# Moving first-layer statistics from VectorE to ScalarE and GpSimd, and a recurrence's cell update to ScalarE

## The chip, the cores and the metric

The kernel runs on one core of one Trainium2 chip. The metric is the time of one execution on the device, in microseconds (us). Five engines of the core work side by side, each through its own instructions in order: TensorE (PE in the profile, its weight loads PEld), VectorE (DVE), ScalarE (ACT), GpSimd (POOL), and SyncE (SP), which here only issues transfers (DMA). An engine that has to wait for another holds up everything queued behind the waiting instruction.

## The reference

The input `x` has 16 images of 128 channels and 64 x 64 points. Two layers are added to it, each after a group normalisation: a diagonal LSTM (a recurrence along the anti-diagonals of the image), and a small simulated quantum circuit on each point. Only the beginning of the first layer matters here.

```python
def _gn(v, G=32, eps=1e-5):
    B_, C_, H_, W_ = v.shape
    g = v.reshape(B_, G, C_ // G, H_, W_)
    m = jnp.mean(g, axis=(2, 3, 4), keepdims=True)
    s = jnp.var(g, axis=(2, 3, 4), keepdims=True)
    return ((g - m) / jnp.sqrt(s + eps)).reshape(v.shape)
...
def step(carry, ist):
    h, c = carry
    h_shift = jnp.pad(h, ((0, 0), (0, 0), (1, 0)))[:, :, :-1]
    s_s = (jnp.einsum('oi,bih->boh', w_ss[:, :, 0], h_shift)
           + jnp.einsum('oi,bih->boh', w_ss[:, :, 1], h) + b_ss[None, :, None])
    gates = ist + s_s
    ofi = jax.nn.sigmoid(gates[:, :3 * C])
    o, f, ig = (ofi[:, :C], ofi[:, C:2 * C], ofi[:, 2 * C:])
    g = jnp.tanh(gates[:, 3 * C:])
    c_new = f * c + ig * g
    h_new = o * jnp.tanh(c_new)
    return ((h_new, c_new), h_new)
...
x = x + _L0_conv_ref(_gn(x), L0_conv_w_is, L0_conv_b_is, L0_conv_w_ss, L0_conv_b_ss)
x = x + _L1_conv_ref(_gn(x), L1_conv_pre_w, L1_conv_pre_b, L1_conv_q_weights, L1_conv_post_w, L1_conv_post_b)
```

So two things must be there before the recurrence can use the images: the mean and variance of every image and group of four channels, and the state of the rows that are not reached yet. A row of the skewed image that waits for its first point sees zeros as input, and its state is the same for every image; it depends only on the weights and on the number of steps.

## The kernel before

The kernel has a preparation, a scan over the diagonals (the LSTM), and a last stage (the circuit and the output). The scan and the last stage are not touched by the change. The preparation loads the 16 images one after another. Of each image, the first 40 rows go to the resident `ring` and the other 24 to seven small buffers (`rest`, three, and four of the `spare` tiles), in pieces of 512 elements per channel (`CHUNK`): eight pieces an image, numbered k = 0 to 7, where k = 0 to 4 lie in the ring.

The order of the work on every engine is the order of the program, since the preparation runs under a hand-written schedule (`manual_schedule`). The parts are these:

- **Statistics** (`statistics`, L285 to L287): one VectorE instruction per piece writes six numbers per channel into `stats` (two halves with count, mean and sum of squared deviations). `aggregated` (L289) makes a mean and a variance per channel of the eight pieces, once per image, into `mv1`.
- **Rounds of the waiting rows** (`inv_step`, L191 to L212): 33 rounds (`EARLY`), each dependent on the one before. TensorE multiplies the state with the summed weights, one product per gate (L199); ScalarE activates the four gates in the order forget, input, candidate, output (L202); GpSimd makes the new cell in three instructions (forget gate times cell L205, input gate times candidate L206, sum L207); ScalarE takes its tanh (L209) and multiplies it with the output gate (L210), which gives the next state `hinv`. Behind each round TensorE has two products whose result nobody reads (`keep`, L182): they only keep it busy, the first of them reads a piece of image b.
- **The loop over images** (L375 to L396) runs two or three rounds per image, then issues the transfers of image b + 2, the statistics of image b + 1 (ring) and of image b (rest), and the aggregation of image b.
- **The seam to the scan** (L400 to L430): GpSimd copies the waiting rows' state into the scan's first state (L402, L403). TensorE then runs, in order, the first gate products of the scan (L408, eight of them in the trace), three products that keep it busy (L416), the mean over each group (L147, from `mv1`), another such product, and the mean of the variances (L426). VectorE and ScalarE form the reciprocal root (L154 to L158), GpSimd normalises the first diagonals (L576 to L588), and the scan starts.

Preparing the circuit's coefficients (`coefficients`, L312 to L319, seven GpSimd instructions) stands ahead of five memsets of the state tiles and one of `w_image` in GpSimd's order. The tile `w_amp` is filled with the circuit's amplitudes later, during the scan, and is not used before.

Of the kernel before, what the change touches and what calls it, by code (L numbers as in the profile page):

```python
# [11 lines left out]
F32 = mybir.dt.float32  # L12
AF = mybir.ActivationFunctionType
# [3 lines left out]
P = 128  # L17
NB = 16
NH = 64
NW = 64  # L20
SLOTS = 32
# [4 lines left out]
BLOCK = ROWS * NW  # L26
CHUNK = 2 * BLOCK
EARLY = 33
FIRST = 8
STRIP = 4  # L30
FEW = 96
# [10 lines left out]
GO, GF, GI, GG = 0, 1, 2, 3  # L42
FUNC = {GO: AF.Sigmoid, GF: AF.Sigmoid, GI: AF.Sigmoid, GG: AF.Tanh}
# [38 lines left out]
def kernel(  # L82
# [16 lines left out]
    nc = tc.nc  # L99
# [36 lines left out]
    def place(r):  # L136

        return (r + AHEAD if r < SLOTS else r - SLOTS) * NW
# [22 lines left out]
    with ExitStack() as scan:  # L161
# [17 lines left out]
        def keep(pool, tag, v):  # L179

            ps = pool.tile([P, v.shape[-1]], F32, name=nc.get_next_instruction_name(), tag=tag)
            nc.tensor.matmul(ps, lhsT=wsT[:, 0:P], rhs=v, start=True, stop=True)  # L182
# [8 lines left out]
        def inv_step(j, pool):  # L191


            ps = {}
            rhs = hinv[:, j : j + 1].to_broadcast([P, P])
            for g in ORDER:
                ps[g] = pool.tile([P, P], F32, name=f"inv_ps{j}_{g}", tag=f"inv{g}")
                w = wsT[:, g * 128 : (g + 1) * 128]
                nc.tensor.matmul(ps[g], lhsT=w, rhs=rhs, start=True, stop=True)  # L199
            ac = small.tile([P, 4], F32, name=f"inv_a{j}", tag="inv_a")  # L200
            for g in ORDER:
                nc.scalar.activation(ac[:, g : g + 1], ps[g][:, 0:1], FUNC[g], bias=bias[:, g : g + 1])  # L202
            ig = small.tile([P, 2], F32, name=f"inv_i{j}", tag="inv_i")
            c = cinv[:, j + 1 : j + 2]
            nc.gpsimd.tensor_mul(ig[:, 0:1], ac[:, GF : GF + 1], cinv[:, j : j + 1])  # L205
            nc.gpsimd.tensor_mul(ig[:, 1:2], ac[:, GI : GI + 1], ac[:, GG : GG + 1])  # L206
            nc.gpsimd.tensor_add(c, ig[:, 0:1], ig[:, 1:2])  # L207
            th = small.tile([P, 1], F32, name=f"inv_t{j}", tag="inv_t")
            nc.scalar.activation(th, c, AF.Tanh)  # L209
            nc.scalar.activation(  # L210
                hinv[:, j + 1 : j + 2], th, AF.Identity, scale=ac[:, GO : GO + 1]
            )  # L212

        def above(v, a, b):

# [4 lines left out]
        with ExitStack() as prep:  # L220
# [64 lines left out]
            def statistics(b, k):  # L285
                v = ring[:, b, k * CHUNK : (k + 1) * CHUNK] if k < 5 else rests[b][k - 5]
                nc.vector.bn_stats(stats[:, b, k, :], v)  # L287

            def aggregated(b):  # L289
                nc.vector.bn_aggr(  # L290
                    mv1[:, b, :], stats[:, b, 0:8].rearrange("p g s -> p (g s)")
                )


            q3 = qw.rearrange("p (n a) -> p a n", a=3)
            ang = pp.tile([P, 2, 3, 8], F32, name="ang")
            rnd = pp.tile([P, 2, 3, 8], F32, name="rnd")
# [14 lines left out]
            def coefficients():  # L312
                nc.gpsimd.tensor_mul(co[:, 0], trig[:, 0, 0, :], trig[:, 0, 2, :])
                nc.gpsimd.tensor_mul(co[:, 1], trig[:, 1, 0, :], trig[:, 0, 2, :])
                nc.gpsimd.tensor_mul(co[:, 2], trig[:, 0, 1, :], trig[:, 1, 2, :])
                nc.gpsimd.tensor_mul(co[:, 3], trig[:, 1, 1, :], trig[:, 1, 2, :])
                nc.gpsimd.tensor_scalar_mul(co[:, 4:8], co[:, 0:4], -1.0)
                nc.gpsimd.tensor_copy(cur[:, 0], expand)
                nc.gpsimd.memset(cur[:, 1], 0.0)  # L319
# [41 lines left out]
                nc.vector.tensor_add(sum_n[:, 2 * i : 2 * i + 2], v[:, :, 0::2], v[:, :, 1::2])  # L361
            transposed("wsT", wsT, lambda g: sum_n[:, g, :])
            biases()
            coefficients()
            for v in (*hst, *xns, none):
                nc.gpsimd.memset(v, 0.0)
            nc.gpsimd.memset(w_image, 0.0)

            for k in (3, 4, 0):
                statistics(0, k)  # L370


            between = [angle_weights, output_weights]
            done = 0
            for b in range(NB):  # L375
                while b < NB - 1 and done * (NB - 1) < EARLY * (b + 1):
                    inv_step(done, ps_inv)
                    keep(ps_keep, "keep", ring[:, b, CHUNK : CHUNK + P])
                    keep(ps_keep, "keep", wsT[:, 0:P])
                    if done == 0:  # L380

                        transposed("wxT", wxT, lambda g: wx_n[:, g, :])
                        transposed("w0T", w0T, lambda g: ws_n[g // 2][:, g % 2, 0::2])
                        transposed("w1T", w1T, lambda g: ws_n[g // 2][:, g % 2, 1::2])
                    elif done > 4 and between:
                        between.pop(0)()
                    done += 1
                if b + 2 < NB:
                    rows(b + 2)
                if b + 1 < NB:  # L390
                    behind(b + 1)
                    for k in ORDERED:
                        statistics(b + 1, k)
                for k in (5, 6, 7):
                    statistics(b, k)
                aggregated(b)  # L396
            prep_ps.close()


# [499 lines left out]
        with tc.manual_schedule():  # L899
# [42 lines left out]

            nc.scalar.activation(warm, shift, AF.Sin)


            def image_weights(i0, i1):
                nc.vector.tensor_mul(
                    w_image[:, i0:i1, 16:32],
# [231 lines left out]
```

## Time and profile before

Three runs took 1410.7, 1411.99 and 1412.01 us, median 1411.99. The profiled execution took 1411.93 us, of which the profile's span is 1409.8 us.

| | busy us | share of the span |
|---|---|---|
| TensorE | 1355.0 | 96% |
| VectorE | 975.5 | 69% |
| GpSimd | 887.6 | 63% |
| ScalarE | 776.0 | 55% |

The page divides the span into 40 slices of about 35 us; a digit is a busy share in tenths. The first three slices are the preparation: transfers at nine tenths in the first two and GB/s of 339, 407 and 234, then almost none until the middle of the scan. A share of busy time over the whole span says nothing about the preparation, whose limits are its own, so it is read in shorter stretches. Among the groups of instructions in the first 125 us, the rounds show as 132 gate activations (mean 262 ns), 33 tanh (203 ns), 33 products with the output gate (294 ns) on ScalarE, and 99 GpSimd instructions of 189 to 193 ns; the statistics as 128 VectorE instructions of 674 to 681 ns and 16 aggregations of 372 ns.

When reading such lines: the time in a line is from the start of its first instruction to the end of its last; the bracket gives the idle time of that engine just before and the instruction that ended it. Neighbouring instructions on ScalarE and GpSimd overlap in the records a little.

### The profile page before, as it was taken

How to read it: one execution, taken by the hardware profiler on the slowest of the kernel's cores; microseconds unless marked ns; L12 is line 12 of the kernel's file. 1: busy time of each engine (PE TensorE's matmuls, PEld its weight loads, DVE VectorE, ACT ScalarE, POOL GpSimd, SP SyncE). 2: the span in 40 equal slices, each digit the busy share in tenths (PEclk: the TensorE clock that was granted, in tenths of full speed). 3: DMA queues.
4: the chain of work that ended last, by engine and by line, in shares of the span. 5: the costliest groups of instructions: out<-in, count | busy, mean ns of one | idle time of the engine just before them, and what ended most of it. 6: DMA issues, size and time to landing. Idle time of an engine off the chain costs nothing.

```text
span 1409.8 us, 20064 instructions
## 1 busy us (share of the span) xinstructions
PE 1355.0 (96%) x6046; PEld 967.6 (69%) x6046; DVE 975.5 (69%) x2541; ACT 776.0 (55%) x1852; POOL 887.6 (63%) x1599
## 2 busy tenths in 40 slices
PE   6778999999999999999999999999999999999995
PEld 5658977777777766666677767777776787886332
DVE  7973565566665666887777776666665567876996
ACT  4655666555555555555555555555555566654331
POOL 4225777777777766777777776777777677763300
PEclk9999999999999999999999999999999999999998
DMA  9960000000000000133333100000000000014999
GB/s 339 407 234 2 1 1 1 1 0 1 0 1 1 1 1 1 60 120 120 120 120 120 60 1 1 1 1 0 1 1 0 1 0 1 1 31 143 383 400 358
DMA packets 64075, 107.04 MB, mean 76 GB/s; under 512 B 5040, under 2 KB 32720, under 8 KB 63968
## 3 DMA queue, kind: packets, MB, share of 16 engines
q1 hardware_dynamic: 59328, 94.39, 18.5%
q0 software_dynamic: 3408, 10.58, 2.0%
q8 instruction: 48, 0.79, 0.2%
q10 hardware_dynamic: 1232, 0.80, 0.2%
q14 instruction: 59, 0.48, 0.1%
HBM read 59.61 MB, written 46.14 MB: 75 GB/s over the span
## 4 chain that ended last, share of the span: by engine, by line
PE 82%; DVE 4%; ACT 1%; issue 1%; POOL 1%; DVEq 0%; ACTq 0%; POOLq 0%
PE ps L783 46%; PE ps L597 28%; PE po_None L1062 3%; PE theta_None L1011 2%; PE am_None L1040 1%; DVE spare L868 1%; DVE ps L858 1%; DVE ps L798 0%; DVE cst L861 0%; DVE stats L732 0%; ACT g L862 0%; ACT g L802 0%; PE po L1062 0%; DVE cst L850 0%; DVE ring L1080 0%
## 5 line engine op out<-in xcount | busy, mean ns | idle before, releaser
L597 PE MATMUL ps<-spare,wxT 128*128 128x512 f32 (+18 forms) x1280 | 479.7, 518 | 0.6 <-POOL spare L588 0.6
L798 DVE TENSOR_TENSOR ps<-ps,both 128x256 f32<-128x256 f32 (+9 forms) x536 | 219.1, 410 | 301.1 <-PE ps L783 299.5
L802 ACT ACTIVATE ps<-ps,bias 128x512 f32<-128x512 f32 (+23 forms) x480 | 279.1, 583 | 221.1 <-DVE ps L798 184.8
L783 PE MATMUL ps<-spare,w1T 128*128 128x256 f32 (+16 forms) x1272 | 346.8, 354 | 9.6 <-DVE spare L759 5.0
L597 PEld LDWEIGHTS ps<-spare,wxT 128*128 128x128 f32 x1280 | 231.1, 190 | 173.0 <-issue 155.4
L783 PE MATMUL ps<-spare,w0T 128*128 128x256 f32 (+16 forms) x1272 | 344.0, 352 | 0.0
L833 ACT COPY both<-ps 128x256 f32<-128x256 f32 (+9 forms) x536 | 189.6, 356 | 181.3 <-PE ps L783 161.7
L783 PEld LDWEIGHTS ps<-spare,w1T 128*128 128x128 f32 x1272 | 230.6, 190 | 36.5 <-DVE spare L868 7.2
L783 PEld LDWEIGHTS ps<-spare,wsT 128*128 128x128 f32 x1088 | 196.1, 190 | 80.4 <-DVE spare L868 30.1
L783 PE MATMUL ps<-spare,wsT 128*128 128x256 f32 (+14 forms) x1088 | 243.9, 366 | 2.6 <-DVE spare L868 1.2
L783 PEld LDWEIGHTS ps<-spare,w0T 128*128 128x128 f32 x1272 | 230.5, 190 | 21.0
L641 POOL TENSOR_TENSOR ring<-ring,spare 128x256 f32<-128x256 f32 (+15 forms) x375 | 231.5, 644 | 17.9 <-DVE spare L868 17.9
L588 POOL TENSOR_TENSOR spare<-spare,rstd 128x512 f32<-128x512 f32 (+10 forms) x160 | 170.9, 1068 | 14.8 <-DVE rstd L158 2.3
L582 POOL TENSOR_TENSOR spare<-ring 128x256 f32<-128x256 f32 (+13 forms) x165 | 139.8, 847 | 0.0
L862 ACT ACTIVATE g<-cst 128x256 f32<-128x256 f32 (+20 forms) x320 | 102.9, 368 | 65.5 <-DVE cst L861 65.1
L868 DVE TENSOR_TENSOR spare<-g,ps 128x256 f32<-128x256 f32 (+17 forms) x319 | 105.3, 368 | 44.8 <-ACT g L862 40.2
L576 POOL TENSOR_TENSOR spare<-ring,mean 128x256 f32<-128x256 f32 (+15 forms) x191 | 122.9, 644 | 5.6 <-DVE mean L148 5.4
L631 POOL TENSOR_TENSOR spare<-spare 128x240 f32<-128x240 f32 (+9 forms) x136 | 102.7, 755 | 36.4 <-DVE spare L868 32.8
L888 POOL COPY spare<-spare 128x16 f32<-128x16 f32 x64 | 21.0, 329 | 150.9 <-DVE spare L868 150.9
L802 ACT ACTIVATE g<-ps,bias 128x512 f32<-128x512 f32 (+20 forms) x160 | 97.3, 608 | 26.6 <-DVE ps L798 20.5
L861 DVE TENSOR_TENSOR cst<-cst,ps 128x256 f32<-128x256 f32 (+20 forms) x320 | 104.6, 368 | 5.5
L858 DVE TENSOR_TENSOR ps<-ps,g 128x512 f32<-128x512 f32 (+20 forms) x160 | 95.0, 594 | 18.8 <-ACT g L802 18.2
(370 smaller groups left out, 1096.4 us busy)
## 6 DMA issues: line engine op xcount, KB each, us to landing
out_dram<-ring SPq DMA_DIRECT2D x93, 256.0 KB, 4.8
ring<-in_x_dram SPq DMA_DIRECT2D x32, 512.0 KB, 7.6
low<-ring SPq DMA_DIRECT2D x6, 2048.0 KB, 7.5
ring<-in_x_dram SPq DMA_DIRECT2D x6, 2048.0 KB, 8.1
spare<-in_x_dram SPq DMA_DIRECT2D x27, 256.0 KB, 6.3
rest<-in_x_dram SPq DMA_DIRECT2D x21, 256.0 KB, 6.4
ring<-low POOLq DMA_DIRECT2D x18, 256.0 KB, 6.7
ring<-in_x_dram SPq DMA_DIRECT2D x16, 256.0 KB, 7.1
```

The lines of the kernel that those rows point to most:

```text
L576: op = nc.gpsimd.tensor_sub(by_pairs(xn, 0, j0, j1), x0, over(mean1, j1 - j0))
L582: op = nc.gpsimd.tensor_sub(by_pairs(xn, 1, j0, j1), lower, of)
L588: nc.gpsimd.tensor_mul(v, v, r)
L597: nc.tensor.matmul(ps[g][:, :, a:b], lhsT=wxT[:, g * 128 : (g + 1) * 128], rhs=xns[t % 2][:, :, a:b], start=t > 0, stop=True, skip_group_c ...
L641: op = engine.tensor_add(x1, x1, by_pairs(new, q, j0, j1))
L783: nc.tensor.matmul(out, lhsT=w[:, g * 128 : (g + 1) * 128], rhs=rhs, start=False, stop=True, skip_group_check=True,)
L798: nc.vector.tensor_add(v, v, both[g][:, a:b])
L802: nc.scalar.activation(to[:, :, a:w], ps[g][:, :, a:w], FUNC[g], bias=bias[:, g : g + 1])
L833: nc.scalar.copy(both[g][:, a:b], ps[g][:, 0, a:b])
L858: nc.vector.tensor_mul(ig, ig, act[GG][:, :, a:w])
L861: nc.vector.tensor_add(c[:, q], c[:, q], ig[:, q])
L868: nc.vector.tensor_mul(new[:, q, a:v], th[:, q, a:v], act[GO][:, q, a:v])
```

## The change

1. In a round, GpSimd keeps one instruction, forget gate times old cell (`kept`), issued right after the forget gate. The new cell is one ScalarE activation: candidate, scaled by the input gate, plus `kept` as bias.
2. The first product that keeps TensorE busy behind a round reads the weights in place of the image.
3. Of images 1 to 4 (`aside`), the statistics of piece k = 0 (rows 32 to 39) are made by ScalarE (`moments_of`): two activations with a running sum (x0 - x and its square, x0 being the first element; their result goes to a PSUM tile that nobody reads), and one that writes the mean into `stats`. GpSimd makes the sum of squared deviations of it.
4. Images 1 to 12 are aggregated by GpSimd, four at a time (`gathering`), in a generator: one piece of one or two instructions after each round (`some`), and whatever is left after the loop. VectorE aggregates images 0, 13, 14 and 15. The scratch space is `w_amp`.
5. `coefficients()` is called behind the memsets and the first statistics.

```diff
@@ inv_step
             ac = small.tile([P, 4], F32, name=f"inv_a{j}", tag="inv_a")
+            kept = small.tile([P, 1], F32, name=f"inv_k{j}", tag="inv_k")
+            c = cinv[:, j + 1 : j + 2]
+            th = small.tile([P, 1], F32, name=f"inv_t{j}", tag="inv_t")
+
+            def activate(to, v, func, **of):
+                nc.scalar.activation(to, v, func, **of)
+
             for g in ORDER:
-                nc.scalar.activation(ac[:, g : g + 1], ps[g][:, 0:1], FUNC[g], bias=bias[:, g : g + 1])
-            ig = small.tile([P, 2], F32, name=f"inv_i{j}", tag="inv_i")
-            c = cinv[:, j + 1 : j + 2]
-            nc.gpsimd.tensor_mul(ig[:, 0:1], ac[:, GF : GF + 1], cinv[:, j : j + 1])
-            nc.gpsimd.tensor_mul(ig[:, 1:2], ac[:, GI : GI + 1], ac[:, GG : GG + 1])
-            nc.gpsimd.tensor_add(c, ig[:, 0:1], ig[:, 1:2])
-            th = small.tile([P, 1], F32, name=f"inv_t{j}", tag="inv_t")
-            nc.scalar.activation(th, c, AF.Tanh)
-            nc.scalar.activation(
-                hinv[:, j + 1 : j + 2], th, AF.Identity, scale=ac[:, GO : GO + 1]
-            )
+                activate(ac[:, g : g + 1], ps[g][:, 0:1], FUNC[g], bias=bias[:, g : g + 1])
+                if g == GF:
+                    nc.gpsimd.tensor_mul(kept, ac[:, GF : GF + 1], cinv[:, j : j + 1])
+            activate(c, ac[:, GG : GG + 1], AF.Identity, scale=ac[:, GI : GI + 1], bias=kept)
+            activate(th, c, AF.Tanh)
+            activate(hinv[:, j + 1 : j + 2], th, AF.Identity, scale=ac[:, GO : GO + 1])
@@ behind aggregated
+            entries = stats[:, :, 0:8].rearrange("p b g (h s) -> p b (g h) s", s=3)
+            aside = range(1, 1 + GATHER)
+            sums1 = w_amp[:, 1, 0 : 2 * NB].rearrange("p (k i) -> p k i", i=NB)
+            gathered, within = (
+                w_amp[:, 0, k * P // 2 : (k + 1) * P // 2].rearrange("p (i e) -> p i e", i=GATHER)
+                for k in range(2)
+            )
+
+            def moments_of(b):
+                at = place(SLOTS)
+                v, x0 = ring[:, b, at : at + CHUNK], ring[:, b, at : at + 1]
+                junk = ps_small.tile([P, CHUNK], F32, name=f"junk{b}", tag="small")
+                for k, func in enumerate((AF.Identity, AF.Square)):
+                    nc.scalar.activation(
+                        junk, v, func, bias=x0, scale=-1.0, accum_out=sums1[:, k, b : b + 1]
+                    )
+                nc.scalar.activation(
+                    entries[:, b, 0:2, 1],
+                    sums1[:, 0, b : b + 1].to_broadcast([P, 2]),
+                    AF.Identity,
+                    bias=x0,
+                    scale=-1.0 / CHUNK,
+                )
+
+            def gathering(b0):
+                b1 = b0 + GATHER
+                pair = [P, GATHER, 2]
+                means, inners = entries[:, b0:b1, :, 1], entries[:, b0:b1, :, 2]
+                s1, s2 = (sums1[:, k, b0:b1] for k in range(2))
+                if b0 in aside:
+                    nc.gpsimd.tensor_mul(s1, s1, s1)
+                    nc.gpsimd.tensor_scalar_mul(s1, s1, -0.5 / CHUNK)
+                    yield
+                    nc.gpsimd.tensor_scalar_mul(s2, s2, 0.5)
+                    nc.gpsimd.tensor_add(
+                        inners[:, :, 0:2], *(v.unsqueeze(2).to_broadcast(pair) for v in (s1, s2))
+                    )
+                    yield
+                m, var = (mv1[:, b0:b1, k] for k in range(2))
+
+                def total(to, v):
+                    n = 8
+                    while n > 1:
+                        nc.gpsimd.tensor_add(gathered[:, :, 0:n], v[:, :, 0:n], v[:, :, n : 2 * n])
+                        v, n = gathered, n // 2
+                        yield
+                    nc.gpsimd.tensor_add(to.unsqueeze(2), v[:, :, 0:1], v[:, :, 1:2])
+                    nc.gpsimd.tensor_scalar_mul(to, to, 1.0 / 16)
+                    yield
+
+                yield from total(m, means)
+                nc.gpsimd.tensor_sub(gathered, means, m.unsqueeze(2).to_broadcast([P, GATHER, 16]))
+                nc.gpsimd.tensor_mul(gathered, gathered, gathered)
+                yield
+                nc.gpsimd.tensor_scalar_mul(within, inners, 1.0 / BLOCK)
+                nc.gpsimd.tensor_add(gathered, gathered, within)
+                yield
+                yield from total(var, gathered)
@@ the preparation
             biases()
-            coefficients()
             for v in (*hst, *xns, none):
                 nc.gpsimd.memset(v, 0.0)
             nc.gpsimd.memset(w_image, 0.0)
             for k in (3, 4, 0):
                 statistics(0, k)
+            coefficients()
             between = [angle_weights, output_weights]
             done = 0
+            behind_pool = []
+
+            def some():
+                for later in behind_pool[:1]:
+                    if next(later, True) is not None:
+                        behind_pool.pop(0)
+
             for b in range(NB):
                 while b < NB - 1 and done * (NB - 1) < EARLY * (b + 1):
                     inv_step(done, ps_inv)
-                    keep(ps_keep, "keep", ring[:, b, CHUNK : CHUNK + P])
+                    some()
+                    keep(ps_keep, "keep", wsT[:, 0:P])
                     keep(ps_keep, "keep", wsT[:, 0:P])
...
+                if b in aside:
+                    moments_of(b)
                 if b + 2 < NB:
                     rows(b + 2)
                 if b + 1 < NB:
                     behind(b + 1)
                     for k in ORDERED:
-                        statistics(b + 1, k)
+                        if k or b + 1 not in aside:
+                            statistics(b + 1, k)
                 for k in (5, 6, 7):
                     statistics(b, k)
-                aggregated(b)
+                if b in (0, *range(13, NB)):
+                    aggregated(b)
+                if b in (5, 9, 13):
+                    behind_pool.append(gathering(b - GATHER))
+            for later in behind_pool:
+                for _ in later:
+                    pass
             prep_ps.close()
```

More of the change, by code (lines that the diff above doesn't have):

```diff
@@ L28 @@
 EARLY = 33
+GATHER = 4
 FIRST = 8
```

## The prediction

> **What bounds the kernel now.** The page first: TensorE is busy 96% of the span and the chain that ended last is 82% TensorE, nearly all of it the scan (L783, L597). The change touches only the preparation before the scan, so I cut the first 150 us into stretches of 10 us. Columns: stretch, its length, then busy us (and instructions) of PE, PEld, DVE, ACT and POOL, granted clock, DMA share, GB/s.
>
> ```profile
> 80.00:90.00 10.00, 7.86 (x51) 6.25 (x50) 9.93 (x19) 5.86 (x25) 2.66 (x14) 1.00 1.04 402
> 90.00:100.00 10.00, 8.02 (x48) 5.66 (x46) 4.48 (x9) 4.64 (x15) 1.60 (x10) 1.00 0.10 37
> ```
>
> Up to 90 us the transfers (1.04) and VectorE (9.93 of 10) both look full. Which of them does the scan wait for? The timeline of each engine at the seam answers (start us, us, engine, line, operation, then idle before it and who ended that):
>
> ```profile
> 94.17 0.37 DVE L290 BATCH_NORM_AGGREGATE mv<-stats 128x2 f32<-128x48 f32 x1
> 100.91 0.17 DVE L148 TENSOR_SCALAR mean<-gm 128x16 f32<-128x16 f32 x1 [6.36 <-PE gm L147]
> ...
> 93.55 0.93 ACT L202 ACTIVATE inv_a<-inv_ps,bias 128x1 f32<-128x1 f32 x4 [0.58 <-PE inv_ps L199]
> 94.83 0.20 ACT L209 ACTIVATE inv_t<-cinv 128x1 f32<-128x1 f32 x1 [0.35 <-POOL cinv L207]
> 95.07 0.29 ACT L210 ACTIVATE hinv<-inv_t,inv_a 128x1 f32<-128x1 f32 x1
> ...
> 93.95 0.19 POOL L205 TENSOR_TENSOR inv_i<-inv_a,cinv 128x1 f32<-128x1 f32 x1 [1.54 <-ACT inv_a L202]
> 94.33 0.19 POOL L206 TENSOR_TENSOR inv_i<-inv_a 128x1 f32<-128x1 f32 x1 [0.19 <-ACT inv_a L202]
> 94.61 0.19 POOL L207 TENSOR_TENSOR cinv<-inv_i 128x1 f32<-128x1 f32 x1
> 94.73 0.20 POOL L402 COPY spare<-hinv 128x16 f32<-128x16 f32 x1
> 95.42 0.19 POOL L402 COPY spare<-hinv 128x1 f32<-128x1 f32 x1 [0.49 <-ACT hinv L210]
> 95.54 0.18 POOL L403 COPY spare<-hinv 128x1 f32<-128x1 f32 x1
> ...
> 94.46 0.49 PE L182 MATMUL I-1329_1330<-wsT 128*128 128x128 f32 x2
> 95.78 0.49 PE L408 MATMUL ps<-spare,w1T 128*128 128x128 f32 x2 [0.83 <-POOL spare L403]
> 97.67 0.81 PE L182 MATMUL I-1369_1370<-rest,wsT 128*128 128x384 f32 x2
> 100.48 0.40 PE L147 MATMUL gm<-mv,wide_sb 128*128 128x16 f32 x2
> ```
>
> VectorE ends at 94.54 and then stands idle 6.36 us: its results enter at the group mean (L147), which TensorE reaches only after the first gate products (L408) and three keep-warm products. That row of TensorE is released by POOL's copies (L403), these by the last round of the waiting rows (L210, ended 95.36). So neither VectorE nor the transfers set the seam; the 33 rounds do. From 21 us on they run with a period of 2.39 us (93.55 against 91.16), one engine after another, and the copies behind them are the gate to the scan. VectorE has about 6 us of slack.
>
> **What the skill says.** The Trainium skill, "ScalarE: Activation LUTs", section "What ACT_TABLE_LOAD costs": 186 ns for an ACTIVATE with immediates, 93 ns more for each pointer operand, 0.833 ns an element, neighbours overlapping by 93 ns. The trace agrees: L209 203 ns, L210 with a pointer scale 294 ns. "TensorE: Matmul & The Clock Gate", Part 1: after a whole idle window of about 3.4 us the array runs at half rate until it has been busy for such a window. Here the eight products of the first round took 2.05 us and those of later rounds 1.16, which fits; no gap later in the run shows a falling back, and the clock column reads 1.00 throughout. "GPSIMD Engine Reference", section 7: reads with a stride over 8 bytes cost about half more per element; at 32 elements the strided L711 (258 ns) against L712 (238) shows it to be small.
>
> **The change, part by part.**
>
> VectorE loses 12 of 16 aggregations (372 ns each, 4.5 us) and 4 of 128 statistics (0.67, 2.7 us): 7.2 us, all in slack. Worth 0. If the rounds were not there it would be worth at most the 3 us or so by which VectorE trails the last transfer.
>
> The round. Before, counted from the start of the forget gate's activation: gates at 0, 0.22, 0.45, 0.67, the last ending at 0.93; POOL's L206 at 0.78, L207 at 1.06, tanh at 1.28. After, the cell is a ScalarE activation behind the fourth gate. In order, it starts about 0.09 before that ends, at 0.84 (the third gate's result is there at 0.71, POOL's one product at 0.60). With scale and bias both pointers it takes 203 + 2 x 91 = 385 ns, an estimate from L209 and L210; end 1.22, tanh at 1.26. Gain 0.02 a round; if the second pointer is free 0.12; if the wait reaches to the fourth gate's end it is 0.10 lost. I take 0.03: 32 rounds, 1 us (bounds: 4 gained, 3 lost). Round 0 gains nothing, since POOL's memsets hold it to 15.2 us; the coefficients move behind these memsets, but their seven instructions stay ahead of round 0 in POOL's queue, so the sum is the same. The first keep-warm product now reads the weights in place of the image: same shape, its wait for a transfer shows no idle time before, 0.
>
> The piece of four images on ScalarE. Each adds two 128x512 activations with sums and a 128x2 one, queued between a round's hinv and the next round's gates, which everything waits for. The nearest row, L1031 (SBUF, 128x512), is 630 ns; with the pointer bias about 0.72. First from 0.20 after hinv's start to 0.92, second (it waits for the first) 0.96 to 1.68, third to 1.88; the next gates start at 1.77 in place of 0.87. TensorE is then ahead, gates follow at 0.15 (as in round 0: four in 0.72) and 0.2 comes back: 0.7 net. Three times 0.7, and 1.1 for the image behind the w_out copy, where there is no idle time to use: 3.2 us. Reading out a sum is not in this trace: between 0 and 0.2 us each; eight of them, I take 0.2 in all. 3.4 us (bounds 2 and 5). The images landed long before, so no wait on transfers.
>
> POOL's aggregation. The generators give out one piece a round, and POOL is idle 1.5 us in each, so during the rounds it is hidden: two instructions (0.75 us) end before the next product is due. But there are three generators of 12, 10 and 10 pieces and, from round 15 on, 18 rounds. The rest is emptied after the loop: in POOL's order 21 instructions stand behind the last round's product and ahead of the copies L402 and L403 (L482, L483 after). Their times from the rows L711 to L715 and the small ones: two scalings of 64 at 0.368, four of 64 at 0.318, three of 32 at 0.245, three of 16 at 0.225, three of 8 at 0.20, six of 4 at 0.19: 5.2 us. 18 wait for the one before, with the 0.085 seen between L206 and L207: 1.5; three overlap by 0.05. Together 6.5 us. The last product ends at 93.55 + 0.59 = 94.14, so POOL is free at 100.7 and the copies end at 101.1, not 95.72: 5.4 us later (bounds 4.5 and 6.5). Queued behind them is L408, and behind that the whole seam on TensorE, in order. What was cheap on VectorE lies bare on POOL.
>
> TensorE idles meanwhile: from 94.95 to 101.1, 6.2 us in place of 0.83. By the skill's window a gap over 3.4 us can drop the rate by half; a free-running window fits whole in 6.2 us with a chance of about 0.8. The seam after it is dense TensorE work, so 3.4 to 6.8 us at half rate lose half of that, 1.7 to 3.4. I take 2.2; bounds 0 and 3.4.
>
> **Sum.** -1 + 3.4 + 5.4 + 2.2 = +10.0 us, all before the scan. On the profiled execution (1411.93 us, span 1409.8 and 2.1 around it) that is 1421.9; the median of the three runs is 1411.99, the same for this purpose, so 1422.
>
> **Rivals.** (a) Tail bare, rest mild: rounds gain their full 4 us, the sums cost 2.5, no half rate: -4 + 2.5 + 5.4 = +4, 1416. For it: no trace here shows the array slowing after a gap. Against: two pointers have their price. (b) Nothing in sum: rounds at 2.2 us (-6) pay for the sums and a tail of 4: about 1412. The in-order start behind the fourth gate speaks against it. (c) The other side: VectorE, full for 55 us, is the true bound, the last statistics let the seam begin, and the tail is hidden behind it. Then 7.2 us less VectorE work, limited by the last transfers (0.10 of the stretch from 90 us, so about 91), brings 2 to 4 us: 1409. The price is VectorE's 0.37 per aggregation, and it decides once VectorE's end lies later than TensorE's arrival at L147. The 9.93 of 10 speaks for it, the 6.36 us of idle time ahead of L148 against. That the work isn't moved at all is excluded by the order of instructions: 4 aggregations remain on VectorE.
>
> **Chances.** Forecast 0.62 (1417 to 1427), (a) 0.17 (1414 to 1417), (b) 0.11, (c) 0.10. A measurement of this kernel tells about 0.2% (2.8 us) from no change: slower 0.77 (the forecast and most of (a)), same 0.13, faster 0.10. The range for 8 in 10 is 1413.5 to 1427.
>
> **What would show it.** Right: POOL works 6 to 7 us after its last product of the rounds; TensorE's first gate products follow the copies after a gap near 6 us, and their eight take over 2.5 us in place of 1.9; four gaps of 1.5 us or more between rounds on ScalarE; VectorE's wait at the group mean grows from 6.4 to over 14 us. Wrong: a round well under 2.3 us, or copies that end within 2 us of the last hinv; then the time is 1412 or less.

## The result, and the profile after

The kernel with the change took 1421.88 us in the median of six runs (1420.85 to 1423.0), the kernel before 1411.38 us beside it. The ratio is 1.0075, with a 95% interval of 1.0062 to 1.0088: 10.5 us slower, as forecast (1422). The profiled execution took 1421.59 us, its span 1419.8 us, against 1411.93 and 1409.8 before.

The stretch of 10 us at the seam, of the kernel after (columns as in the prediction: busy us and instructions of PE, PEld, DVE, ACT, POOL, then granted clock, DMA share, GB/s):

```profile
100.00:110.00 10.00, 5.59 (x20) 4.21 (x20) 0.00 (x0) 0.00 (x0) 3.43 (x15) 0.66 0.00 0
```

Between 100 and 110 us VectorE and ScalarE do nothing at all, GpSimd works a third of the time, and TensorE runs for part of it at a granted clock of 0.66. The timeline of the kernel after, by engine, says why (start us, us, engine, line, operation; in brackets the idle time before and who ended it):

```profile
94.23 0.37 DVE L293 BATCH_NORM_AGGREGATE mv<-stats 128x2 f32<-128x48 f32 x1
111.65 0.17 DVE L149 TENSOR_SCALAR mean<-gm 128x16 f32<-128x16 f32 x1 [17.05 <-PE gm L148]
...
97.90 0.29 ACT L207 ACTIVATE hinv<-inv_t,inv_a 128x1 f32<-128x1 f32 x1
...
96.92 0.41 POOL L352 TENSOR_SCALAR w_amp<-stats 128x64 f32<-128x64 f32 x1
...
103.58 0.22 POOL L345 TENSOR_SCALAR mv<-mv 128x4 f32<-128x4 f32 x1
103.86 0.32 POOL L482 COPY spare<-hinv 128x16 f32<-128x16 f32 x2
104.12 0.18 POOL L483 COPY spare<-hinv 128x1 f32<-128x1 f32 x1
...
97.34 0.49 PE L183 MATMUL I-1323_1324<-wsT 128*128 128x128 f32 x2
104.35 0.80 PE L488 MATMUL ps<-spare,w1T 128*128 128x128 f32 x2 [6.52 <-POOL spare L483]
104.94 0.64 PE L488 MATMUL ps<-spare,w0T 128*128 128x128 f32 x2
...
107.93 1.29 PE L183 MATMUL I-1382_1383<-rest,wsT 128*128 128x384 f32 x2
109.28 0.91 PE L183 MATMUL I-1385_1386<-rest,wsT 128*128 128x384 f32 x2
111.22 0.40 PE L148 MATMUL gm<-mv,wide_sb 128*128 128x16 f32 x2
```

Three times are to be set against those of before. The last hidden vector ends at 98.19 (before 95.36): +2.83. The first gate products start at 104.35 (95.78): +8.57, since GpSimd first empties its aggregation, from 96.92 to 103.80. The group mean starts at 111.22 (100.48): +10.74, since a pair of gate products now takes 0.64 us where it took 0.39, and the first keep product 1.29 where the second, of the same shape, takes 0.91. After this the distance roughly stays: 11.0 us at 120 us, 10.4 at the start of the last stage, 10.0 at the end of the span. What brought the last 0.7 us back in this execution stays open.

One thing is to be known for all comparisons of times with traces. The device time is longer than the span by 2.1 us in every execution of the kernels with the old rounds, and by 1.8 us in every one of the kernels with the new cell update (before: 1411.93 and 1409.8; after: 1421.59 and 1419.8). Why isn't known. So the 10.5 us of the medians are about 10.8 within the span, which is what the group mean shows.

VectorE's last aggregate ends at 94.60 (before 94.54), though it has 7.2 us less to do: it waits for the transfers instead. Its waits for pieces of images between 15 and 95 us sum to 7.3 us, against 1.7 before.

The time on ScalarE, first in the groups between 20 and 112 us (busy us, mean ns), then the timeline around the sums of image 1, both of the kernel after:

```profile
L207 ACT ACTIVATE cinv<-inv_a,inv_k 128x1 f32<-128x1 f32 x32 | 12.1, 377 | 0.1
L311 ACT ACTIVATE junk<-ring 128x512 f32<-128x512 f32 x8 | 5.5, 685 | 0.1
L311 ACT ACTIVATION_READ_ACCUMULATOR junk<-ring 128x1 f32 x8 | 1.5, 186 | 0.0
```

```profile
27.48 0.29 ACT L207 ACTIVATE hinv<-inv_t,inv_a 128x1 f32<-128x1 f32 x1
27.68 0.67 ACT L311 ACTIVATE junk<-ring 128x512 f32<-128x512 f32 x1
28.29 0.18 ACT L311 ACTIVATION_READ_ACCUMULATOR junk<-ring 128x1 f32 x1
...
29.42 0.69 ACT L207 ACTIVATE inv_a<-inv_ps,bias 128x1 f32<-128x1 f32 x4
```

From the start of `hinv` to the next gates it is 1.94 us here (two sums with their read-outs and a small activation for the mean, L314, lie between); before it was 0.87 (27.56 to 28.43). The four gates then take 0.69 in place of 0.93, since TensorE is ahead. From this hidden vector to the next it is 3.22 us (27.48 to 30.70); rounds without sums have a period of 2.345 us (gates at 94.09 and 96.43), in place of 2.39 before. So a set of sums costs a net 0.88 us.

### The profile page after: what moved, and what is told of

Read it like the earlier page. It is cut to its first block, busy times and chain, and to the rows that moved or that the text cites. A ratio compares the mean times of both kernels' runs of the same rounds, so it can differ in the third digit from the quotient of the medians.

```text
span 1419.8 us, 20084 instructions
## 1 busy us (share of the span) xinstructions
PE 1357.1 (96%) x6046; PEld 968.6 (68%) x6046; DVE 970.5 (68%) x2525; ACT 791.1 (56%) x1905; POOL 885.8 (62%) x1579
## 3 DMA queue, kind: packets, MB, share of 16 engines
q1 hardware_dynamic: 59328, 94.39, 18.3%
## 4 chain that ended last, share of the span: by engine, by line
PE 80%; DVE 5%; ACT 2%; issue 1%; POOL 1%; DVEq 0%; ACTq 0%; POOLq 0%
PE ps L863 45%; PE ps L677 28%; PE po_None L1141 3%; PE theta_None L1090 2%; PE am_None L1119 1%; DVE stats L812 1%; DVE spare L948 1%; DVE ps L938 1%; ACT ps L882 1%; DVE ps L878 1%; DVE cst L941 1%; ACT g L882 1%; ACT g L942 0%; PE po L1141 0%; DVE ring L1159 0%
```

## The experiments

The theory was the prediction's: the gate to the scan is the chain of rounds, copies, gate products and group mean; the change lengthens it by sums on ScalarE, by GpSimd's emptying ahead of the copies, and by half rate on TensorE after the gap; VectorE's relief is worth nothing. The first experiments take away one of these each. All diffs of the first four are against the kernel after, and so are the differences of medians given with them. The kernel before took 1411.85 us beside these four and 1411.38 beside the kernel after; measured from the kernel before, each of them gains 0.5 us more.

**Keeping TensorE busy in the gap.** Six products of 384 columns are put where it stood idle.

```diff
+            for _ in range(6):
+                keep(ps_keep, "keep", wxT[:, 0 : 3 * P])
             prep_ps.close()
```

> The changed kernel with six more products of 384 columns (result unread) on TensorE between the last round and the first gate products. Theory (the array falls to half rate in the 6.5 us gap, and that costs the 6.9 us instead of 4.7 us from the first gate products to the group mean): the eight gate products take 1.9 us again instead of 3.6, the clock reads 1.00 in the stretch from 100 to 110 us, the copies still end near 104.3 us, and the kernel is 2.2 us faster than the change, near 1419.7. Rival (the gap costs only its own length, and the slow products have another cause, such as GpSimd's traffic): no change, 1421.9, products still near 3.6 us.

Measured: 1420.56 us, ratio to the kernel before 1.0059 (1.0045 to 1.0073). The timeline and the window of this kernel at the seam:

```profile
104.71 0.49 PE L490 MATMUL ps<-spare,w1T 128*128 128x128 f32 x2 [0.68 <-POOL spare L485]
105.03 0.39 PE L490 MATMUL ps<-spare,w0T 128*128 128x128 f32 x2
```

```profile
100.00:110.00 10.00, 8.92 (x34) 4.39 (x34) 0.16 (x1) 0.00 (x0) 3.67 (x16) 1.00 0.00 0
```

The gate products come as late as before the edit, but a pair takes 0.39 us again, the clock reads 1.00, and from the first of them to the group mean it is 4.70 us, exactly as in the kernel before, not 6.87. So in the seam half rate costs 2.17 us, and idle time is its cause. In the medians only 1.3 us of that arrive (1.8 when each is measured from the kernel before beside it), and the two intervals overlap: the trace shows the gain, the time alone does not. Part of what is missing is in the same trace. Behind the sums of image 2 TensorE fell to half rate here, which it did not in the profiled execution of the kernel after, and that round takes 3.14 us in place of 2.345 (more in the last section).

**No emptying behind the last round.** Two pieces a round, and only images 1 to 8 on GpSimd (VectorE aggregates 9 to 12 again).

```diff
                     some()
+                    some()
...
-                if b in (0, *range(13, NB)):
+                if b in (0, *range(9, NB)):
                     aggregated(b)
-                if b in (5, 9, 13):
+                if b in (5, 9):
                     behind_pool.append(gathering(b - GATHER))
```

> The changed kernel with two pieces of aggregation after each round instead of one, and the third group of four images (9 to 12) aggregated by VectorE as before, so that nothing is left to GpSimd after the last round. Theory (the bare tail delays the copies by 5.75 us and the idle array costs 2.2 more): 7.9 us faster than the change, near 1414, that is 2.5 to 3 us slower than the kernel before, with the copies ending 0.4 us after the last hinv. Rival (VectorE's end sets the seam): its four aggregations come back at 0.37 us each, so the gain is at least 1.5 us smaller, 1415.5 or more.

Measured: 1414.41 us (14 runs), ratio 1.0016 (1.0008 to 1.0024). In its timeline the copies follow the last hidden vector at once:

```profile
98.37 0.29 ACT L207 ACTIVATE hinv<-inv_t,inv_a 128x1 f32<-128x1 f32 x1
...
98.85 0.18 POOL L484 COPY spare<-hinv 128x1 f32<-128x1 f32 x1
```

The copies end 0.37 us after the hidden vector (after the change: 6.11; before it: 0.36), TensorE has no gap that matters, the group mean starts at 103.78, and 7.5 us are gone. What is left of the change, rounds and sums, costs the 2.6 us by which this kernel stays above the 1411.85 us of the kernel before; the prediction's terms for these were -1 and +3.4.

**The copies ahead of the emptying.** The same work, but the loop that empties the generators stands behind the copies.

```diff
-            for later in behind_pool:
-                for _ in later:
-                    pass
             prep_ps.close()
...
             nc.gpsimd.tensor_copy(hst[0][:, 1, NB : NB + 1], hinv[:, EARLY : EARLY + 1])
+            for later in behind_pool:
+                for _ in later:
+                    pass
```

> The changed kernel with the same work in another order: the rest of the aggregation is issued on GpSimd behind the copies of the waiting rows' state instead of ahead of them. Theory: the first gate products start near 98.6 us and run beside the rest of the aggregation, the group mean waits for it until about 104.5 us instead of 111.2, [...]the kernel is 6.5 us faster than the change, near 1415.4. Rival (the aggregation's length, and not its place, is what counts): 0 to 2 us faster.

Measured: 1413.9 us (21 runs), ratio 1.0015 (1.0008 to 1.0021): 8.0 us faster by order alone, more than expected. GpSimd's and TensorE's timeline of this kernel:

```profile
98.87 0.18 POOL L480 COPY spare<-hinv 128x1 f32<-128x1 f32 x1
...
101.73 0.22 POOL L345 TENSOR_SCALAR mv<-mv 128x4 f32<-128x4 f32 x1
...
104.77 0.25 POOL L345 TENSOR_SCALAR mv<-mv 128x4 f32<-128x4 f32 x1
...
103.85 0.37 PE L148 MATMUL gm<-mv,wide_sb 128*128 128x16 f32 x2
```

GpSimd still works until 105.02, but the group mean reads only means. The last of these is done at 101.95, the group mean follows TensorE's own queue at 103.85, and for the last variances VectorE waits about 0.1 us. The expectation had counted a wait there that doesn't exist. So it was the place of the emptying, not its length, that cost.

**No sums on ScalarE.** VectorE takes the four pieces back (`gathering` then skips their two steps).

```diff
-            aside = range(1, 1 + GATHER)
+            aside = ()
```

> The changed kernel with the pieces of images 1 to 4 back on VectorE, nothing else different. Theory (each set of sums holds back the next round's gates by 0.9 us net, one by 1.3): the last hinv comes near 94.2 us instead of 98.2, and the kernel is 4 us faster than the change, near 1418; the tail behind the last round is the same length. Rival (ScalarE's sums fit into its idle time between rounds and VectorE is what they relieve): equal or slower by up to 2.7 us, 1422 to 1424.5.

Measured: 1415.57 us, ratio 1.0025 (1.0015 to 1.0036): 6.3 us less than with them, not 4. The rounds gave what was expected: the last hidden vector ends at 94.51 (-3.7), although this execution began its rounds 0.48 us later. From the third hidden vector to the last it is 70.95 us in place of 75.11, so the sums cost 4.2 us. The claim that the tail keeps its length was wrong: without the two extra pieces 18 instructions are left for the end in place of 21, and the copies end 4.86 us behind the hidden vector, not 6.11 (-1.25). The stretch at half rate is shorter too, as the timeline shows:

```profile
99.42 0.80 PE L488 MATMUL ps<-spare,w1T 128*128 128x128 f32 x2 [5.28 <-POOL spare L483]
...
102.14 0.54 PE L488 MATMUL ps<-spare,w1T 128*128 128x128 f32 x2
102.52 0.39 PE L488 MATMUL ps<-spare,w0T 128*128 128x128 f32 x2
```

Full rate is back within the gate products, 3.1 us after the first of them, where the kernel after needed 4.5: from the first gate product to the group mean 6.13 us, not 6.87 (-0.74). The three together are 5.7 us, or 6.2 without the later beginning.

The next two stand against the kernel before, and try the parts that should help.

**The cell update alone.**

```diff
-            nc.gpsimd.tensor_mul(ig[:, 0:1], ac[:, GF : GF + 1], cinv[:, j : j + 1])
-            nc.gpsimd.tensor_mul(ig[:, 1:2], ac[:, GI : GI + 1], ac[:, GG : GG + 1])
-            nc.gpsimd.tensor_add(c, ig[:, 0:1], ig[:, 1:2])
...
+                if g == GF:
+                    nc.gpsimd.tensor_mul(kept, ac[:, GF : GF + 1], cinv[:, j : j + 1])
+            activate(c, ac[:, GG : GG + 1], AF.Identity, scale=ac[:, GI : GI + 1], bias=kept)
```

> The kernel before with one thing of the change alone: the cell update of the rounds on ScalarE (the product of the forget gate on GpSimd, then one activation with scale and bias in place of GpSimd's product and sum). Theory: it is the only part that helps, by the 0.045 us that the changed kernel's period (2.345 us) is shorter than the one before (2.39 us), 33 rounds of it: the last hidden vector 1.4 us earlier (95.36 to about 93.9), copies and first gate products too. VectorE ends at 94.54 us and the group mean comes only after the gate products and three keep products, so all of it should arrive: 1410.4 us, between 1409.8 and 1411. Rival: the gain is lost at the group mean or later, because something other than the rounds ends last there: 1411.5 to 1412, no difference.

Measured: 1409.13 us (20 runs) beside 1411.4, ratio 0.9984 (0.9978 to 0.9991), so 1.3 to 3.1 us faster: the expected 1.4 lies just inside, the median of 2.3 is more. Of these 2.3 us, 0.3 lie outside the span (1.8 around it in place of 2.1). In its trace the last hidden vector ends 2.25 us earlier. From the third round's products to those of the last it is 70.93 us (19.89 to 90.82) against 72.29 (20.73 to 93.02): 1.36 us, the whole of what was expected. The rest of the 2.25 was there before the third round. The second round's products in the two timelines, first the kernel before, then this one:

```profile
17.79 1.91 PE L199 MATMUL inv_ps<-hinv,wsT 128*128 128x128 f32 x8
```

```profile
17.54 1.06 PE L199 MATMUL inv_ps<-hinv,wsT 128*128 128x128 f32 x8
```

In one execution TensorE still ran at half speed there, in the other not any more. This doesn't follow the code: the kernels after and without sums have the slow second round as well, the one with TensorE kept busy and the one with the copies first have the fast one; and of the four versions of the seam below, whose code is the same up to the last round, two have the slow one and two the fast one. Single traces of this preparation thus differ by some 0.9 to 1.1 us for no reason in their code. (The kernels before and after, as compared above, both have the slow one.) How often each kernel has which can't be told from one trace each, so what the median gains beyond the 1.4 of the rounds and the 0.3 outside the span stays open.

**VectorE relieved alone.**

```diff
+            nc.gpsimd.memset(mv1, 1.0)
...
-                        statistics(b + 1, k)
+                        if k or b + 1 not in range(1, 5):
+                            statistics(b + 1, k)
...
-                aggregated(b)
+                if b in (0, *range(13, NB)):
+                    aggregated(b)
```

> The kernel before without twelve of the sixteen aggregations and four of the statistics on VectorE (about 7 us of its work, what the change takes off it); the means and variances of those images are set to 1.0 at the start, so this leaves out part of the statistics. The rounds are those before. Theory: VectorE is no bound for the first stage: its work ends with the last transfers, and the group mean waits for TensorE. Period of the rounds 2.39 us, last hidden vector at 95.4, group mean at 100.5, total within 1 us of the kernel before. Rival (the third of the prediction): VectorE, 99% busy, is the true bound, and relief of it brings 2 to 4 us by itself: 1408 to 1410.

Measured: 1411.0 us (13 runs), ratio 0.9998 (0.999 to 1.0006). Its VectorE timeline:

```profile
93.73 0.37 DVE L291 BATCH_NORM_AGGREGATE mv<-stats 128x2 f32<-128x48 f32 x1
100.25 0.17 DVE L148 TENSOR_SCALAR mean<-gm 128x16 f32<-128x16 f32 x1 [6.14 <-PE gm L147]
```

VectorE ends 0.44 us earlier and waits about as long as before, although this execution has the fast second round and reaches its group mean 0.67 us earlier (99.81). A unit that is 99% busy for 55 us was not the bound; the change saved time where none was short.

**Shortening the seam itself.** If the chain at the seam is the bound, it can be cut directly. On top of the cell update alone, first the three keep products ahead of the group mean are dropped:

```diff
-            for v in (rests[NB - 2][0], rests[NB - 2][2], rests[NB - 1][0]):
-                keep(ps_small, "small", v[:, 0 : 3 * P])
```

> The cell update on ScalarE alone, and in addition the three keep products of 384 columns between the first gate products and the group mean left out. Theory: the group mean stands behind them on TensorE's queue and its statistics are ready (VectorE's last aggregate ends at 94.5 us), so they are on the path: 2.8 us more than the cell update alone, 1407.6 us, group mean at about 96.3. TensorE is not idle for longer than 1 us, so no half rate. Rival: without them something else ends last (VectorE's last aggregate or ScalarE's table load), or TensorE falls to half rate: 1409.5 to 1411.

Measured: 1405.81 us, ratio 0.996 (0.9947 to 0.9972): 3.3 us below the cell update alone. In its trace (the slowest of the five executions, with the slow second round) the group mean at 96.60 follows the eight gate products without a gap; TensorE's longest idle time there is 0.78 us and it stays at full rate.

Then, in another version, the group mean and VectorE's variance go ahead of the gate products, the variance's product behind them, and no keep product is left between:

```diff
+            group_mean(ps_small, mv1[:, :, 0], mean1, 1, 1.0)
...
             first = {}
...
-            for v in (rests[NB - 2][0], rests[NB - 2][2], rests[NB - 1][0]):
-                keep(ps_small, "small", v[:, 0 : 3 * P])
-
-            group_mean(ps_small, mv1[:, :, 0], mean1, 1, 1.0)
...
-            keep(ps_gate, "gate", wxT[:, 0 : 3 * P])
```

> The cell update on ScalarE alone, and in addition the group mean's product and VectorE's variance put ahead of the copies' gate products, the variance's product right behind these, and no keep product between. Theory: the group mean can start when VectorE's last aggregate is done (94.5 us), so mean and variance run beside the copies and the eight gate products (1.9 us); the variance's product at about 96.5 in place of 101.8, the first normalised products at about 98.7 in place of 104.0, total about 5 us below the kernel before, 1406 to 1407. Rival: the gates then wait behind the group mean by more than is won, or the stage behind it waits for other things (the second group's table loads, the first gates): 1409 to 1411.

Measured: 1407.24 us (1404.84 to 1408.61), ratio 0.9966 (0.9953 to 0.9978). Faster than the kernel before, but not better than the last. TensorE's timeline and windows of 1 us of this kernel:

```profile
94.62 0.61 PE L147 MATMUL gm<-mv,wide_sb 128*128 128x16 f32 x2 [2.01 <-DVE mv L292]
95.07 0.78 PE L415 MATMUL ps<-spare,w1T 128*128 128x128 f32 x2
95.64 0.63 PE L415 MATMUL ps<-spare,w0T 128*128 128x128 f32 x2
```

```profile
94.00:95.00 1.00, 0.38 (x2) 0.38 (x2) 0.54 (x2) 0.28 (x1) 0.00 (x0) 0.64 0.00 0
95.00:96.00 1.00, 1.00 (x6) 1.00 (x6) 0.63 (x4) 0.00 (x0) 0.23 (x1) 0.50 0.00 0
```

The clock falls to 0.50 at about 94.3 (0.64 is the mean of 0.28 us at 1 and 0.72 at 0.5), 1.7 us after the last product (which ended at 92.62), and the gate products pay for it: the variance's product starts at 98.62, not 96.5. In the next run one keep product bridges the wait for VectorE:

```diff
+            keep(ps_small, "small", wxT[:, 0 : 3 * P])
             group_mean(ps_small, mv1[:, :, 0], mean1, 1, 1.0)
```

> The kernel with the group mean and variance ahead of the first gate products (stats first), and one keep product of 384 columns between the last round's products and the group mean's. Without it TensorE stood idle for 2.01 us there, and the eight gate products took 3.55 us (98.62 less 95.07) where 1.89 us were expected. Theory: that idle time threw TensorE to half rate; the keep product (0.91 us) cuts the gap to about 1.0 us, the gate products take 1.9 us again, the granted clock stays at 1.00, and the time falls by the 1.7 us: about 1405.6 us, between 1404.8 and 1406.5. Rival: the slow gate products have another cause (variance products and gate products sharing something), or the gap of 1 us is enough: 1407 us as without it, granted clock 0.7 in that stretch.

Measured: 1406.48 us, ratio 0.9962 (0.995 to 0.9975). The eight gate products take 1.86 us again (95.38 to 97.24) and the clock reads 1.00: the same products in the same order run at full rate, so it was the rate and not the order that slowed them. That the keep product kept the rate isn't shown by this trace. It has the slow second round, its rounds end 1.76 us later than those of the run before, and VectorE's last aggregate (95.06) comes only 0.7 us behind the last round's products (94.39), so the gap would have been short without it too. The gain of 0.8 us in the medians (1.4 measured from the kernel before beside each) is less than expected and too small for five runs to tell from none.

Last, the variance's product is put between the fourth and the fifth gate product:

```diff
             for g in ORDER:
+                if g == ORDER[2]:
+                    gv = ps_small.tile([P, NB], F32, name="gv1", tag="small")
+                    nc.tensor.matmul(gv, lhsT=group, rhs=var, start=True, stop=True)
...
```

> As the bridged kernel, with the variance's product after four of the eight first gate products in place of after all eight. Theory: VectorE has the variance ready about 0.6 us after the mean (three operations of 0.17 us), when four products are through, so the variance's product comes 0.9 us earlier and the reciprocal root, GpSimd's normalisation and the next products with it: 0.9 us below the bridged kernel, about 1404.7 us. Rival: VectorE's chain isn't ready so early, so TensorE waits and the gate products are held up, or the stage behind waits for the last gate products anyway: within 0.5 us of the bridged kernel or slower.

Measured: 1405.26 us (1404.09 to 1408.46) beside 1412.03, ratio 0.9959 (0.9945 to 0.9972). VectorE's last aggregate and TensorE's timeline in its trace, which has the fast second round:

```profile
94.68 0.37 DVE L292 BATCH_NORM_AGGREGATE mv<-stats 128x2 f32<-128x48 f32 x1
...
95.15 0.37 PE L147 MATMUL gm<-mv,wide_sb 128*128 128x16 f32 x2 [1.69 <-issue]
...
96.41 0.40 PE L416 MATMUL gv<-var,wide_sb 128*128 128x16 f32 x2
```

The variance's product starts at 96.41 (bridged: 97.24), and the first normalised products at 98.71 (99.36; before the change 103.98). The step is in the trace; in the medians the three best versions, 1405.3, 1405.8 and 1406.5 us, can't be told apart. All are about 0.4% faster than the kernel before, by means of one part of the change and a seam that has nothing to do with the rest of it.

With this order VectorE does come last: its aggregate is done at 95.05, the copies were done at 93.54, and the group mean starts at 95.15. ("issue" in its line means that the profile shows nothing that TensorE waited for; by the program it reads this aggregate.) So VectorE is no bound in the order of the kernel before, and is one in this order. Whether less work on VectorE would help here wasn't tried; in the two kernels that take 7 us from it, it ended at 94.60 and 94.10 in place of 94.54, since it waits for transfers, so half a microsecond is the most that can be expected (an estimate).

## Why the prediction was right

**What bounds the kernel.** Shown. The seam follows the rounds: without VectorE's work nothing changes (the run with VectorE relieved), with a shorter chain at the seam the whole kernel gets shorter (the last four). Rival (c), VectorE as the true bound, is refuted for the order of the kernel before.

**The round** (-1): the period fell by 0.045 us, 1.4 us over the rounds. The new cell activation took 377 ns where 385 was estimated from two neighbours, and both pointers have their price. The gain was put at 0.03. The step behind it was right: the cell starts behind the fourth gate, 0.83 us after the first (0.84 forecast). Rivals (a) and (b) both needed 2.2 to 2.27 us a round, which didn't come.

**The sums** (+3.4): the hidden vector's delay of 2.83 us plus the 1.4 that the rounds gain is 4.2 us, and the run without sums gives 4.2 too. This term was mis-sized by 0.8 us. Read off the rounds it is three times 0.88 and 1.3 for the image behind the `w_out` copy, 3.9 to 4, and one round in the middle (the 18th) that takes 2.60 us in place of 2.345; that round is late in all four traces with sums and not in the run without, and its cause stays open. The prediction took 0.2 us in all for reading out the sums; the read-out is an instruction of its own, 186 ns, eight times. The upper bound of the term (5) covered it. What no term had: the sums also leave TensorE idle for up to 1.73 us, which in two of the four traces brought half rate among the rounds (last section).

**GpSimd's tail** (+5.4): the copies end 6.11 us behind the last hidden vector in place of 0.36, so +5.75. The count of 21 instructions was right; 6.5 us were estimated for them, and 6.88 measured (96.92 to 103.80). Two runs confirm the term as a cause: with the tail gone, or only behind the copies, 7.5 to 8.0 us vanish, against the 7.6 that were forecast for this term and the next together (7.9 in the traces).

**Half rate after the gap** (+2.2): 2.17 us, taken away whole by products that fill the gap. The mechanism came from the Trainium skill, "TensorE: Matmul & The Clock Gate", Part 1, which puts the array at half rate after at least one idle window of about 3.4 us; the gap of 6.5 us was beyond it, and the clock fell in it. The prediction's reading that the clock column of the kernel before reads 1.00 throughout holds for the stretches up to 150 us; in the last slice of the page PEclk is 8, and from 1396 us, behind the last products, it reads 0.50, so the fall could have been seen. That the size came within 0.03 us is luck: the term was a guess between 0 and 3.4, and the similar gap of the run without sums (5.3 us) cost 1.43. The same page's advice, in "Why this matters for your kernels", to leave no gaps over some 3 us is too generous here: a gap of 2.0 us was enough in one run, and one of 1.7 in two others.

**The sum**: 10.0 was forecast and 10.5 measured in the medians; 10.74 at the group mean. The errors of the terms (-0.4, +0.8, +0.35, 0) are inside their bounds, and together they are the 0.75 us that the group mean is later than forecast. So nothing is left at the seam for the two parts that were put at nothing and not tried alone, the other operand of the keep product and the place of `coefficients`. That the sum came closer than its worst term is in part luck, since the error of the rounds goes the other way.

## What to carry to other kernels

An engine that is 99% busy is not the bound if what it makes is waited for by nobody: look at the first instruction that reads its results, and at who released that one, and look again when the order is changed. Work that is moved to an idle engine is free only while it stands behind nothing urgent in that engine's queue; if it must be emptied somewhere, empty it behind the instructions that release others, which here was worth 8.0 us for the same work. And a gap on TensorE can cost twice, once as idle time and once in the products that follow.

## What was not expected of the hardware

An activation with a running sum is followed by an instruction of its own that reads the sum out (186 ns for 128x1).

At the seam TensorE lost its full rate over gaps of 6.5, 5.3 and 2.0 us, and kept it over gaps of 0.8 us and one of 1.7 (ahead of the group mean in the last run). Among the rounds, the same gap went both ways. Behind the sums of image 2 TensorE waits 1.73 us in all four traces with sums. First the round that follows in the kernel after, then in the run with TensorE kept busy, with two of its windows:

```profile
37.61 1.16 PE L200 MATMUL inv_ps<-hinv,wsT 128*128 128x128 f32 x8 [1.73 <-ACT hinv L207]
```

```profile
37.18 1.95 PE L200 MATMUL inv_ps<-hinv,wsT 128*128 128x128 f32 x8 [1.73 <-ACT hinv L207]
...
37.00:38.00 1.00, 0.82 (x4) 0.82 (x5) 1.00 (x3) 0.24 (x2) 0.00 (x0) 0.68 1.04 418
38.00:39.00 1.00, 1.00 (x7) 1.00 (x6) 1.00 (x3) 0.67 (x3) 0.19 (x1) 0.50 1.03 420
```

The run without the tail kept its rate there too, the run with the copies first lost it (eight products in 2.08 us). In these two the round takes 3.14 and 3.26 us in place of 2.345, so this is 0.8 to 0.9 us more in one execution than in another.

What decides isn't the length of the gap alone: the clock fell 4.2 us after the last product in the kernel after, and 1.7 us after it in the run with the group mean first. It stayed at half rate for 3.4 us in the two runs with the fall among the rounds, 3.5 in the run without sums, and 6.8 in the kernel after and in the run with the group mean first. In the kernel after, the windows of 1 us show both ends:

```profile
102.00:103.00 1.00, 0.00 (x0) 0.00 (x0) 0.00 (x0) 0.00 (x0) 0.77 (x3) 0.54 0.00 0
...
108.00:109.00 1.00, 1.00 (x3) 0.27 (x2) 0.00 (x0) 0.00 (x0) 0.00 (x0) 0.55 0.00 0
```

It fell at about 102.1 and was back at about 108.9, 6.8 us later, 4.5 of them under load. The column doesn't show the case of the second round: between 17 and 19 us of the kernel before it reads 1.00, while the eight products of the second round take 1.91 us in place of 1.06. Durations of products of one shape are the surer sign.
